# A macaron block (FFN, neighbourhood attention, FFN): the fourth tile's first norm and FFN ahead of the first values, the attention bias's parts earlier, eleven second FFNs held back, and the last norms' products on VectorE

## The chip, the cores and the metric

The kernel runs on one core of one Trainium2 chip. The metric is device time in microseconds (us): of the version before there are three timed runs, 2368.54, 2367.49 and 2367.25, median 2367.49, and one profiled run of 2366.79, whose recorded span is 2365.0. Every duration below comes from that one profiled execution.

A core has a matrix engine (PE in the profile, TensorE), a vector engine (DVE, VectorE), an activation engine (ACT, ScalarE), a general engine (POOL, GpSimd) and a queue that issues transfers (SP, SyncE). Each works through its own list of instructions strictly in order; semaphores tie them together.

## The reference

The input is x, 4 batches of 4096 rows of 512 floats. Cut to what matters:

```python
x = x + 0.5 * ffn(layernorm(x))
x = x + attention(layernorm(x))
x = x + 0.5 * ffn(layernorm(x))

def ffn(x):                     # one 512x512 weight
    xq, xs = mx_quantize(x)     # blocks of 32: scale = max|x|/7.5, values to the FP6-E2M3 grid
    wq, ws = mx_quantize(weight)
    return dequant(xq, xs) @ dequant(wq, ws).T + bias

def attention(x):               # 16 heads of 32, each query sees 13 neighbours
    q, k, v = split(x @ qkv_w.T + qkv_b); q *= 32 ** -0.5
    attn = softmax(q @ k[neighbours].T + rpb[relative position])
    return (attn @ v[neighbours]) @ proj_w.T + proj_b
```

## The kernel before

The 16384 rows are 128 tiles of 128 rows (NT). Four tiles are a group (512 rows), eight groups a batch. What a tile does: load; norm "n1", quantised; first FFN ("f1", its sum in PSUM is pmf); norm "n2"; values (pmv). What a group does, in four items, one for every four heads: queries and keys (pmqk), scores (ps), softmax, probabilities times values (pv), collected in a buffer `ring`. Then each tile again: output projection (pmo); norm "n3", quantised; second FFN ("f2", also pmf); store.

Nearly f32 precision comes from pairs of f16: every operand is kept as a high part and a low part, and `product` (L151) runs three combinations of parts times four chunks of 128, which makes 12 matmuls of 128x512. A high part is a copy on ACT (L200), a low part a subtraction on VectorE (L204), after which SP issues a transposing DMA (L205); xT is what it delivers to the FFN's product.

A quantised norm is made in one stage after another by `quantised_norms`: factors from mean and variance (POOL, L186 to L195), scaled rows y (ACT, L233), block maxima, scales and reciprocals (VectorE, L239 to L244), y times reciprocal (POOL, L246), cast to 8 bits (ACT, L249), times scale (POOL, L251), high part (ACT, L200), low part (VectorE, L204) and transposing DMA. Norms enlisted for the same slot are made as one pair (128x1024 in place of 128x512). For the last tiles a flag `spare`, true from tile 123 on, lets the stage take its buffers from the pool of the tiles (xp, 23 buffers) and not from the norms' own few buffers.

The order is written out by hand. `begin(slot, stage, rank)` puts a stage into a numbered slot, `run_slot` emits a slot's stages by rank, and a stage is a generator that yields how many slots later it goes on. A tile takes STEP = 7 slots; with k = 7t, a tile is loaded at k-18, its norm n1 is enlisted at k-10, `first_half` (first FFN and norm n2) begins at k+5 (F1), `values` at k+20 (V). An attention item takes 7 slots too: pmqk at +38, scores at +42, pv at +59. The output projection of tile t stands at `out_slot(t)`, its norm n3 two slots later, its second FFN at `second_slot(t)`. n1 of tile t and n3 of an earlier tile mostly fall in one slot, and are a pair.

At the start the weights are quantised and transposed ("setup"); 16 chunks of weights are put in place (`put_scaled`, L789 ACT and L791 VectorE, names whl) at listed slots up to 35, and `attention_bias` (its operand vbx at L821 and L822, its product pmb) begins at slot 28. Tiles 0 to 2 have their first norms inside the setup (EARLY = 3); tile 3 is the first whose n1 runs by the slots.

At the end there is too little other work between the last attention items. So eight second FFNs are kept back: HELD (L582) is tiles 113 to 120, and `second_slot` spreads their products over the slots around the last scores and pv. Their transposed operand xT is put in an xp buffer, to wait there. After the last pv come five output projections (tiles 123 to 127) and the last second FFNs.

Of the kernel before, what the change touches and what calls it, by code (L numbers as in the profile page):

```python
# [27 lines left out]
F16 = mybir.dt.float16  # L28
# [4 lines left out]
ALU = mybir.AluOpType  # L33
# [4 lines left out]
P = 128  # L38
# [7 lines left out]
GROUP = 4  # L46
# [4 lines left out]
QB = 32  # L51
# [13 lines left out]
def macaron_kernel(  # L65
# [12 lines left out]
    nc = tc.nc  # L78
# [3 lines left out]
    KC = dim // P  # L82
# [3 lines left out]
    NT = n_batch * length // P  # L86
# [15 lines left out]
    x2p = ctx.enter_context(tc.tile_pool(name="x2p", bufs=2))  # L102
# [17 lines left out]
    half_ffn_b = const.tile([P, dim], F32, name="half_ffn_b")  # L120
# [8 lines left out]
    def bc(t, n):  # L129

        return t.unsqueeze(2).to_broadcast([t.shape[0], t.shape[1], n])
# [30 lines left out]
    def begin(slot, stage, rank=5):  # L162
        slots.setdefault(slot, []).append((rank, stage))
# [19 lines left out]
    def factors(t, which, mv, n=1):  # L183

        rs = sm.tile([P, n], F32, tag=f"rs{which}{n}", name=f"rs{which}_{t}")
        nc.gpsimd.tensor_scalar(  # L186
            rs, mv[:, :n, 1], XS ** -2, LN_EPS * XS ** -2, ALU.mult, ALU.add
        )
        nc.gpsimd.tensor_tensor(rs, rs, minus_half[:, :n], ALU.pow)
        nb = sm.tile([P, n], F32, tag=f"nb{which}{n}", name=f"nb{which}_{t}")  # L190
        if n == 1:
            nc.gpsimd.tensor_scalar(nb, mv[:, 0, 0:1], rs, -1.0, ALU.mult, ALU.mult)  # L192
        else:
            nc.gpsimd.tensor_tensor(nb, mv[:, :n, 0], rs, ALU.mult)
            nc.gpsimd.tensor_scalar(nb, nb, -1.0, None, ALU.mult)  # L195
        return rs, nb

    def high(y, hl):

        nc.scalar.copy(hl[:, :, 0, :], y)  # L200
# [5 lines left out]

    together = {}

    def enlist(slot, t, which):
        together.setdefault(slot, ([], []))[0].append((t, which))
# [7 lines left out]
    def quantised_norms(slot):  # L220

        tiles, mv = together.pop(slot)
        n = len(tiles)
        rs, nb = factors(slot, "q", mv[0], n)
        yield 1, 1

        spare = tiles[0][0] >= NT - GROUP - 1
        if spare:
            y = xp.tile([P, dim], F32, tag="x", name=f"yq{slot}").unsqueeze(1)
        else:  # L230
            y = yp.tile([P, 2, dim], F32, tag="yq", bufs=2, name=f"yq{slot}")[:, :n]
        for u, (t, _) in enumerate(tiles):
            nc.scalar.activation(  # L233
                y[:, u], xs[t], AF.Identity, bias=nb[:, u : u + 1], scale=rs[:, u : u + 1]
            )
        yield 1, 1
        yb = y.rearrange("p u (n q) -> p (u n) q", q=QB)
        sc = sm.tile([P, 2 * NB], F32, tag="sc", bufs=4, name=f"sc{slot}")[:, : n * NB]
        nc.vector.tensor_reduce(sc, yb, AX.X, ALU.max, apply_absolute_value=True)  # L239
        nc.vector.scalar_tensor_tensor(  # L240
            sc, sc, F8_SCALE / Q_MAX, least[:, : n * NB], ALU.mult, ALU.max
        )
        r = sm.tile([P, 2 * NB], F32, tag="r", bufs=4, name=f"r{slot}")[:, : n * NB]
        nc.vector.reciprocal(r, sc)  # L244
        yield 1, 1
        nc.gpsimd.tensor_tensor(yb, yb, bc(r, QB), ALU.mult)  # L246
        yield 1, 1
        q8 = q8p.tile([P, 2, dim], F8, tag="q8", name=f"q8_{slot}")[:, :n]
        nc.scalar.activation(q8, y, AF.Identity, bias=nudge, saturate=False)  # L249
        yield 1, 3  # L250
        nc.gpsimd.tensor_tensor(  # L251
            yb, q8.rearrange("p u (n q) -> p (u n) q", q=QB), bc(sc, QB), ALU.mult
        )
        yield 1, 3
        if spare:
            hl = xp.tile([P, dim], F32, tag="x", name=f"hlq{slot}").bitcast(F16)
            hl = hl.rearrange("p (u s k) -> p u s k", u=1, s=2)
        else:
            hl = hlp.tile([P, 2, 2, dim], F16, tag="hlq", name=f"hlq{slot}")[:, :n]
        high(y, hl)  # L260
        yield 1, 1
        if tiles[0][0] in HELD and tiles[0][1] == "n3":
            xT = xp.tile([P, dim], F32, tag="x", name=f"xT{slot}").bitcast(F16)
            xT = xT.rearrange("p (u s c q) -> p u s c q", u=1, s=2, c=KC)
        else:
            xT = xtp.tile([P, 2, 2, KC, P], F16, tag="xT", name=f"xT{slot}")
        low(y, hl, xT[:, :n].rearrange("p u s c q -> p (u s c) q"))
        for u, (t, _) in enumerate(tiles):
            ys[t] = xT[:, u]
# [11 lines left out]
    def first_half(t):  # L281

        yield from ffn(t, "f1")
        yield 1, 2
        mv = sm.tile([P, 1, 2], F32, tag="mvn2", name=f"mvn2_{t}")
        statistics(t, "n2", mv[:, 0, :])
        yield 1, 2
        rs, nb = factors(t, "n2", mv)
        yield 1, 2
        y = yp.tile([P, 1, dim], F32, tag="yn2", bufs=1, name=f"yn2_{t}")  # L290
        nc.scalar.activation(y[:, 0], xs[t], AF.Identity, bias=nb, scale=rs)
        hl = hlp.tile([P, 1, 2, dim], F16, tag="hln2", name=f"hln2_{t}")
        high(y, hl)
        yield 2, 2
        g, i = divmod(t, GROUP)
        if i == 0:
            x2[g] = x2p.tile([P, 2, KC, GROUP, P], F16, tag="x2", name=f"x2_{g}")
        low(y, hl, x2[g][:, :, :, i, :].rearrange("p s c q -> p (s c) q"))

    x2 = {}  # L300
# [44 lines left out]
    n_items = n_batch * NG * KC  # L345
# [204 lines left out]
    def project_out(t, slot):  # L550

        r = t * P % RING
        pm = ps_m.tile([P, dim], F32, tag="mm", name=f"pmo_{t}")
        product(
            pm, lambda s, c: ring[:, s, c, r : r + P], lambda s, c: wt[:, s, c, PO : PO + dim]
        )
        yield 1, 8
        nc.vector.scalar_tensor_tensor(xs[t], pm, cp, xs[t], ALU.mult, ALU.add)
        moments(slot, t, "n3")
# [7 lines left out]
    EARLY = 3  # L567
    STEP = 7

    F1, V, QK, SC, PV, OUT, F2 = 5, 2 * STEP + 6, 5 * STEP + 3, 6 * STEP, 8 * STEP + 3, 13 * STEP + 2, 12  # L570
# [4 lines left out]
    def one(f, *args):  # L575
        f(*args)
        return
        yield

    HELD = range(NT - 15, NT - 7)  # L582
    LAST = NT - GROUP - 1

    def out_slot(t):


        i = t - LAST
        if i >= 0:
            return (n_items - 1) * STEP + PV + 3 + 2 * i  # L590
        if i >= 1 - GROUP:
            return LAST * STEP + PV + 21 + 4 * i
        return t * STEP + OUT

    def second_slot(t):

        i = t - LAST
        if t in HELD:
            return (n_items - 1) * STEP + PV - (16, 13, 10, 6, 5, 4, 3, 2)[t - HELD[0]]
        if i in (-2, -1):  # L600
            return out_slot(NT - 1) + 3 + i
        return out_slot(t) + F2

    for t in range(NT):
        k = t * STEP
        begin(k - 18, one(load, t), 0)
        enlist(k - 10, t, "n1")
        if not 0 < t < EARLY:
            begin(k - 11, one(moments, k - 10, t, "n1"), 1)
        begin(k + F1, first_half(t))  # L610
        begin(k + V, values(t))
        begin(k + F1, one(add_bias, t, half_ffn_b), 8)
        at = out_slot(t)
        begin(at - 5, one(add_bias, t, after_b), 8)
        enlist(at + 2, t, "n3")
        begin(at, project_out(t, at + 2))
        begin(at + 6 if t < LAST else second_slot(t) - 2, one(add_bias, t, half_ffn_b), 8)
        begin(second_slot(t), second_half(t))
    for slot in together:
        if slot >= EARLY * STEP - 10:  # L620
            begin(slot, quantised_norms(slot), 1)
    for m in range(n_items):
        k = m * STEP
# [3 lines left out]
    for n in range(n_batch * NG):  # L627
        k = n * GROUP * STEP
        b, g = divmod(n, NG)
# [4 lines left out]
    with tc.tile_pool(name="setup", bufs=1) as sp, tc.tile_pool(name="scratch", bufs=2) as scr:  # L634
# [21 lines left out]
        for o in chunks:  # L656
            w, i = (qkv_w, o) if o < 3 * KC else (proj_w, o - 3 * KC)
# [160 lines left out]
        def attention_bias():  # L818

            vbx = sp.tile([P, 2, KC, P], F16, name="vbx")  # L820
            nc.scalar.copy(vbx[:, 0], bc(vb, P))  # L821
            nc.vector.tensor_tensor(vbx[:, 1], bc(vb, P), vbx[:, 0], ALU.subtract)  # L822
            yield 3, 9
            pmb = ps_m.tile([P, dim], F32, tag="mm", name="pmb")
            product(pmb, lambda s, c: vbx[:, s, c, :], lambda s, c: wt[:, s, c, PO : PO + dim])
            yield 1, 9
            nc.vector.scalar_tensor_tensor(after_b, pmb, cp, after_b, ALU.mult, ALU.add)
# [42 lines left out]
        begin(0, one(scales), 9)  # L870
        for slot, o in zip((2, 4, 5, 6, 10, 13, 16, 19, 21, 23, 25, 27, 29, 31, 33, 35), chunks):
            begin(slot, put_scaled(o), 9)
        begin(28, attention_bias(), 9)
        begin(26, one(put_table), 9)
        slot = first
        while slot < QK:
# [47 lines left out]
```

## Time and profile before

| what | value | where it is from |
| --- | --- | --- |
| timed runs | 2367.25, 2367.49, 2368.54 us | median 2367.49 |
| profiled run | 2366.79 us | 0.70 below the median |
| its span | 2365.0 us | 1.79 us of the run lie around it |
| PE not busy | 91.4 us | 2365.0 less 2273.6 busy |
| granted clock of the PE, mean | 0.994 | cores view |
| busy from 120 to 2240 us | PE 99.9% | sum of the stretches in the view by windows |

Times are microseconds from the start of the span. In the view of single instructions a line reads: start, duration, engine, line of the kernel, operation, result<-operands, shape, number of instructions in the row; in brackets the idle time just before it and whose result ended it. In the view by windows a line gives the stretch, its length, then busy time and (in brackets) instructions of PE, PE's weight loads, VectorE, ACT and POOL, then the clock granted to the PE (1.00 is full), the mean busy share of the DMA engines, and GB/s. The chain of waits follows the work that ended last back to the start.

The PE idles in two places only: in the first 106 us, and in the last 105 us.

### The profile page before, as it was taken

How to read it: one execution, taken by the hardware profiler on the slowest of the kernel's cores; microseconds unless marked ns; L12 is line 12 of the kernel's file. 1: busy time of each engine (PE TensorE's matmuls, PEld its weight loads, DVE VectorE, ACT ScalarE, POOL GpSimd, SP SyncE). 2: the span in 40 equal slices, each digit the busy share in tenths (PEclk: the TensorE clock that was granted, in tenths of full speed). 3: DMA queues.
4: the chain of work that ended last, by engine and by line, in shares of the span. 5: the costliest groups of instructions: out<-in, count | busy, mean ns of one | idle time of the engine just before them, and what ended most of it. 6: DMA issues, size and time to landing. Idle time of an engine off the chain costs nothing.

```text
span 2365.0 us, 82328 instructions
## 1 busy us (share of the span) xinstructions
PE 2273.6 (96%) x35539; PEld 1115.4 (47%) x35539; DVE 2022.5 (86%) x3588; ACT 1326.8 (56%) x2080; POOL 1987.6 (84%) x2012
## 2 busy tenths in 40 slices
PE   0799999999999999999999999999999999999988
PEld 0255444444444444444444444444444444444543
DVE  8799888888888888888888888888888888888785
ACT  4466556555555555555555565555555555555542
POOL 5588888888888888888888888888888888888886
PEclk9899999999999999999999999999999999999999
DMA  5789787787777777777777778777777778677763
GB/s 154 146 168 165 156 160 155 147 159 156 151 157 152 156 158 153 156 152 158 153 157 153 153 159 154 153 154 156 158 151 160 151 152 160 153 152 155 133 121 104
DMA packets 925701, 360.59 MB, mean 152 GB/s; under 512 B 718876, under 2 KB 889752, under 8 KB 925336
## 3 DMA queue, kind: packets, MB, share of 16 engines
q1 hardware_dynamic: 924992, 354.79, 73.3%
q8 instruction: 278, 4.55, 0.9%
q10 hardware_dynamic: 344, 0.53, 0.1%
q14 instruction: 87, 0.71, 0.1%
HBM read 110.15 MB, written 67.29 MB: 75 GB/s over the span
## 4 chain that ended last, share of the span: by engine, by line
PE 94%; DVE 3%; DMA 1%; POOL 1%; issue 1%; ACT 0%; SPq 0%; DVEq 0%; ACTq 0%; POOLq 0%
PE pmqk L151 28%; PE pmf L151 27%; PE pmo L151 14%; PE pmv L151 14%; PE ps L442 7%; PE pv L512 3%; DVE fw L761 0%; DMA xT<-hlq 0%; DMA fw<-in_L_ffn_weight_dram 0%; DVE stn L180 0%; DVE wq L763 0%; DVE hlq L204 0%; DVE wqh L757 0%; DMA rows<-in_L_attn_qkv_w_dram 0%; DVE whl L791 0%
## 5 line engine op out<-in xcount | busy, mean ns | idle before, releaser
L151 PE MATMUL pmf<-wt,xT 128*128 128x512 f16 x3048 | 703.5, 381 | 9.1 <-DMA xT<-hlq 9.1
L151 PE MATMUL pmqk<-x,wt 128*128 128x512 f16 x3072 | 705.7, 379 | 1.4 <-DVE vt L315 1.4
L151 PEld LDWEIGHTS <-xT 128*128 128x128 f16 x3048 | 299.1, 98 | 373.7 <-DMA xT<-hlq 11.5
L151 PEld LDWEIGHTS <-wt 128*128 128x128 f16 x3072 | 289.6, 98 | 336.6 <-issue 1.9
L151 PE MATMUL pmv<-wt,x 128*128 128x512 f16 x1536 | 355.0, 381 | 5.1 <-DVE mvn L181 5.1
L246 POOL TENSOR_TENSOR yq<-yq,r 128x1024 f32<-128x1024 f32 (+1 forms) x141 | 246.5, 1748 | 130.0 <-DVE r L244 130.0
L151 PE MATMUL pmo<-wt,ring 128*128 128x512 f16 x1536 | 354.8, 381 | 0.8 <-issue 0.8
L573 POOL TENSOR_TENSOR x<-x,half_ffn_b 128x512 f32<-128x512 f32 x256 | 327.4, 1279 | 0.1
L279 DVE SCALAR_TENSOR_TENSOR x<-pmf,coef,x 128x512 f32<-128x512 f32 x256 | 179.7, 702 | 156.4 <-PE pmf L151 155.9
L314 ACT CAST vt<-pmv 128x512 f16<-128x512 f32 x128 | 74.9, 585 | 388.9 <-PE pmv L151 388.9
L539 ACT ACTIVATE ring<-pv 128x510 f16<-128x510 f32 (+8 forms) x224 | 82.3, 414 | 368.4 <-PE pv L512 368.4
L180 DVE BATCH_NORM_STATS2 stn<-x 128x6 f32<-128x512 f32 x384 | 265.3, 691 | 8.9 <-DMA x<-in_L_attn_x_dram 0.2
L251 POOL TENSOR_TENSOR yq<-q,sc 128x1024 f32<-128x1024 fp8e4 (+1 forms) x141 | 246.7, 1749 | 0.0
L151 PEld LDWEIGHTS <-x 128*128 128x128 f16 x1536 | 150.8, 98 | 188.1 <-DMA x<-hln 5.6
L377 DVE SCALAR_TENSOR_TENSOR qk<-pmqk,qk_b,qk 128x512 f16<-128x512 f32 x256 | 190.5, 744 | 42.2 <-ACT qk L373 41.1
L151 PEld LDWEIGHTS <-ring 128*128 128x128 f16 x1536 | 140.7, 98 | 159.4 <-issue 3.3
L249 ACT ACTIVATE q<-yq,nudge 128x1024 fp8e4<-128x1024 f32 (+1 forms) x141 | 149.9, 1063 | 114.3 <-POOL yq L246 106.1
L485 POOL TENSOR_TENSOR sf<-sf,total 128x714 f32<-128x714 f32 (+2 forms) x128 | 178.6, 1395 | 34.5 <-ACT yq L233 19.1
L373 ACT ACTIVATE qk<-pmqk,qk_b 128x512 f16<-128x512 f32 x256 | 176.1, 688 | 52.1 <-PE pmqk L151 50.8
L186 POOL TENSOR_SCALAR rsq<-mv 128x2 f32<-128x2 f32 (+1 forms) x141 | 130.1, 923 | 89.3 <-DVE mv L181 86.6
L233 ACT ACTIVATE yq<-x,nbq,rsq 128x512 f32<-128x512 f32 x254 | 193.0, 804 | 18.0 <-POOL nbq L192 17.5
L492 POOL TENSOR_TENSOR p<-sf,p 128x714 f16<-128x714 f32 (+2 forms) x128 | 192.6, 1504 | 0.0
(145 smaller groups left out, 3459.7 us busy)
## 6 DMA issues: line engine op xcount, KB each, us to landing
vs<-vd SPq DMA_DIRECT2D x144, 357.0 KB
x<-in_L_attn_x_dram SPq DMA_DIRECT2D x128, 256.0 KB
vd<-vt SPq DMA_DIRECT2D x128, 256.0 KB
out_dram<-x SPq DMA_DIRECT2D x128, 256.0 KB
vs<-vd SPq DMA_DIRECT2D x24, 378.0 KB
vs<-vd SPq DMA_DIRECT2D x24, 315.0 KB
rows<-in_L_attn_qkv_w_dram SPq DMA_DIRECT2D x12, 256.0 KB
xT<-hlq SPq DMA_TRANSPOSE x141
```

Of the source, the lines that this page charges most:

```text
L151: nc.tensor.matmul(pm, lhs(a, c), rhs(b, c), start=(n == 0), stop=(n == 3 * KC - 1))
L180: nc.vector.bn_stats(st, xs[t])
L233: nc.scalar.activation(y[:, u], xs[t], AF.Identity, bias=nb[:, u : u + 1], scale=rs[:, u : u + 1])
L246: nc.gpsimd.tensor_tensor(yb, yb, bc(r, QB), ALU.mult)
L251: nc.gpsimd.tensor_tensor(yb, q8.rearrange("p u (n q) -> p (u n) q", q=QB), bc(sc, QB), ALU.mult)
L279: nc.vector.scalar_tensor_tensor(xs[t], pm, cf, xs[t], ALU.mult, ALU.add)
L373: nc.scalar.activation(t[:, s, 0, KN:], pms[s], AF.Identity, bias=bias)
L377: nc.vector.scalar_tensor_tensor(t[:, s, 1, KN:], pms[s], bias, t[:, s, 0, KN:], ALU.add, ALU.subtract)
L442: nc.tensor.matmul(ps[rows, u, :sides, w * KN : (w + 1) * KN], t[rows, 0, part, q0 : q0 + QR], t[rows, 1, :sides, k0 : k0 + KN], start=par ...
L485: nc.gpsimd.tensor_tensor(s, s, bc(total[:, :n], KN), ALU.mult)
L492: nc.gpsimd.tensor_tensor(p[:, :n, KN : 2 * KN], s, ph, ALU.subtract)
L573: nc.gpsimd.tensor_tensor(xs[t], xs[t], b, ALU.add)
```

## The change

1. Tile 3 is treated like tiles 0 to 2: it is loaded in the same slot as tile 2, its n1 stands at slot 1 and not 11, and the `first_half` of tiles 0 to 3, with the bias additions that belong to it, begins 0, 2, 5 and 7 slots sooner. PE's list then begins pmf0, pmf1, pmf2, pmf3, pmv0, pmv1, pmb, pmf4, pmv2, pmqk0, where it was pmf0, pmf1, pmf2, pmv0, pmf3, pmv1, pmb, pmf4, pmv2, pmqk0. From there on the lists agree until item 119.
2. `attention_bias` makes vbx at slot 20 and not 28; its product stays at slot 31.
3. HELD is tiles 110 to 120, eleven and not eight. Ten of them have new slots around the last pv; tile 120 goes behind all output projections, seven slots after the last. On PE's list the second FFNs of 110, 111 and 112 no longer stand ahead of the scores of items 119, 120 and 121; behind the last scores (item 127) the list reads pmf110, pmo, pv, pmf111, pmo, pmf112, 113, 114, pv, pmf115 to 119, pv, five pmo, pmf121, 122, 123, 124, 120, 125, 126, 127. Before it was pmf113, pmo, pv, pmf114, pmo, pmf115, pv, pmf116 to 120, pv, five pmo, pmf121 to 127.
4. Held tiles from 115 on keep their xT in two buffers of the pool x2p, not in xp.
5. The norm n3 of a held tile is enlisted one slot later, so that it is not paired with an n1 any more. In particular the n1 of tiles 125, 126 and 127 stand alone, and as their first tile is over 122 they count as spare.
6. In spare norms (n1 of 125 to 127, n3 of 123 to 127) the two products, with the reciprocal and with the scale, are made by VectorE and not by POOL.

```diff
+    held = []
...
-        nc.gpsimd.tensor_tensor(yb, yb, bc(r, QB), ALU.mult)
+        mult = nc.vector if spare else nc.gpsimd
+        mult.tensor_tensor(yb, yb, bc(r, QB), ALU.mult)
...
-        nc.gpsimd.tensor_tensor(
+        mult.tensor_tensor(
             yb, q8.rearrange("p u (n q) -> p (u n) q", q=QB), bc(sc, QB), ALU.mult
         )
...
-        if tiles[0][0] in HELD and tiles[0][1] == "n3":
+        t0 = tiles[0][0]
+        is_held = t0 in HELD and tiles[0][1] == "n3"
+        if is_held and t0 >= NT - 13:
+            g, i = divmod(t0 - (NT - 13), GROUP)
+            if i == 0:
+                held.append(x2p.tile([P, 2, KC, GROUP, P], F16, tag="x2", name=f"held{g}"))
+            xT = held[g][:, :, :, i, :].unsqueeze(1)
+        elif is_held:
...
-    HELD = range(NT - 15, NT - 7)
+    HELD = range(NT - 18, NT - 7)
...
+        if t == HELD[-1]:
+            return out_slot(NT - 1) + 7
         if t in HELD:
-            return (n_items - 1) * STEP + PV - (16, 13, 10, 6, 5, 4, 3, 2)[t - HELD[0]]
+            return (n_items - 1) * STEP + PV - (16, 13, 10, 9, 8, 6, 5, 4, 3, 2)[t - HELD[0]]
...
     for t in range(NT):
         k = t * STEP
-        begin(k - 18, one(load, t), 0)
-        enlist(k - 10, t, "n1")
+        sooner = (0, 2, 5, STEP)[t] if t <= EARLY else 0
+        begin(k - 18 - (STEP if t == EARLY else 0), one(load, t), 0)
+        slot = k - 10 - (10 if t == EARLY else 0)
+        enlist(slot, t, "n1")
         if not 0 < t < EARLY:
-            begin(k - 11, one(moments, k - 10, t, "n1"), 1)
-        begin(k + F1, first_half(t))
+            begin(slot - 1, one(moments, slot, t, "n1"), 1)
+        begin(k + F1 - sooner, first_half(t))
         begin(k + V, values(t))
-        begin(k + F1, one(add_bias, t, half_ffn_b), 8)
+        begin(k + F1 - sooner, one(add_bias, t, half_ffn_b), 8)
         at = out_slot(t)
         begin(at - 5, one(add_bias, t, after_b), 8)
-        enlist(at + 2, t, "n3")
-        begin(at, project_out(t, at + 2))
+        n3 = at + (3 if t in HELD else 2)
+        enlist(n3, t, "n3")
+        begin(at, project_out(t, n3))
...
     for slot in together:
-        if slot >= EARLY * STEP - 10:
+        if together[slot][0][0][1] == "n3" or together[slot][0][0][0] >= EARLY:
             begin(slot, quantised_norms(slot), 1)
...
-            yield 3, 9
+            yield 11, 9
...
-        begin(28, attention_bias(), 9)
+        begin(20, attention_bias(), 9)
```

## The prediction

> **What bounds the kernel now.** First the page: busy time and the chain.
>
> ```profile
> PE 2273.6 (96%) x35539; PEld 1115.4 (47%) x35539; DVE 2022.5 (86%) x3588; ACT 1326.8 (56%) x2080; POOL 1987.6 (84%) x2012
> PE 94%; DVE 3%; DMA 1%; POOL 1%; issue 1%; ACT 0%; SPq 0%; DVEq 0%; ACTq 0%; POOLq 0%
> ```
>
> PE sets the end, and the two programs give it equally many instructions. So only PE's 91.4 us of idleness and its cold stretches can be had. The view by windows says where they are:
>
> ```profile
> 20.00:40.00 20.00, 0.37 (x1) 0.08 (x1) 20.00 (x31) 7.24 (x19) 15.81 (x12) 1.00 0.18 54
> 80.00:100.00 20.00, 12.45 (x41) 4.66 (x42) 18.23 (x33) 10.29 (x16) 10.84 (x17) 0.74 0.80 165
> 2260.00:2280.00 20.00, 17.79 (x415) 9.21 (x415) 15.71 (x32) 9.37 (x15) 17.76 (x17) 0.91 0.56 101
> 2300.00:2320.00 20.00, 15.33 (x131) 6.79 (x130) 14.22 (x24) 7.03 (x13) 18.47 (x18) 0.83 0.72 168
> ```
>
> From 20 to 40 VectorE is full (20.00 of 20.00, setup); at 80 PE has 12.45 of 20 and a clock of 0.74; near the end it idles again. PE's own timeline names each wait:
>
> ```profile
> 72.92 5.30 PE L151 MATMUL pmv<-wt,x 128*128 128x512 f16 x12 [5.10 <-DVE mvn L181]
> 82.49 4.24 PE L151 MATMUL pmf<-wt,xT 128*128 128x512 f16 x12 [4.27 <-DMA xT<-hlq]
> 86.56 2.75 PE L151 MATMUL pmv<-wt,x 128*128 128x512 f16 x12
> ...
> 98.80 2.94 PE L151 MATMUL pmf<-wt,xT 128*128 128x512 f16 x12
> ...
> 2272.20 1.34 PE L442 MATMUL ps<-qk 32*32 32x84 f16 x144 [2.15 <-DVE qk L377]
> 2273.48 4.42 PE L151 MATMUL pmo<-wt,ring 128*128 128x512 f16 x12
> ...
> 2306.32 0.83 PE L512 MATMUL pv<-pT,vs 126*32 126x30 f16 x72 [4.67 <-DMA vs<-vd]
> ...
> 2351.39 9.63 PE L151 MATMUL pmf<-wt,xT 128*128 128x512 f16 x36 [2.53 <-DMA xT<-hlq]
> ```
>
> A warm product (12 matmuls) takes 2.60 from start to start, 4.2 to 5.3 behind an idle spell. The last two items wait 2.14 and 2.15 for VectorE's low part of the keys, pv then 4.67, and the last FFNs 0.39, 1.93 and 2.53.
>
> **The head.** Tile 3's norm joins the setup. By the starts of a later tile's rows (moments 64.00, 64.72, 64.82; maximum, scale, reciprocal 70.22, 70.93, 71.14, 71.31) that is 0.72 + 0.10 + 0.71 + 0.21 + 0.17 = 1.9 on the full VectorE, and 1.55 where instructions of other work stand between these, since a 512-wide one then takes 0.6 from start to start. Its low part (0.60) falls into the 6.22 in which VectorE waits for pmf0 (56.4 to 62.67), its two products into POOL's free 4.2 of the stretch from 20 to 40. The setup is interleaved, so pmf0 comes 1.5 later; at least 0.6 (some falls behind 40, where VectorE has 3.7 of 20 free), at most 2.5 (dependent steps, and the low part in front of pmf0 after all: 1.9 + 0.6). SP issues one more transpose and one earlier load there; its queue is not what pmf0 waits for (that is the weights' transposing).
>
> Then pmf3 follows pmf2 at once and no longer stands in pmv0's and pmv1's way. Before, its xT came at 82.49 (L204 at 77.43, 1.76 long, then 3.3 for the transpose). I lay the same instructions out in the new lists, with the durations of their rows: pmv0 still at 73, pmv1 78.6 (was 86.56), x3 complete at 82.0 (was 92.58), pmb 87.5, bound by the last projection weights (was 90.51 and 95.41: vbx is now early, so the 1.19 and 3.86 for it go), the low part for pmf4 at 89.5 and pmf4 at 94.05 (was 98.80: 4.75 sooner). Behind it pmqk0 at 99.4 (105.73) and first scores at 110.5 (116.18): 5.7 sooner. I take 4.7, as pmf4's own, since pmqk0 also needs tile 3's n2 chain. vbx moved eight slots ahead costs VectorE 0.6 ahead of x2's moments, already in the layout. Net: 1.5 - 4.7 = -3.2 (-5.1 to 0). From 116 to 2170 PE has no wait to speak of, so all of it is carried through.
>
> **The tail, first part.** Without pmf110, 111, 112 three periods of an item hold 15.0 of PE's work, not 17.6: 3 x 2.60 = 7.8 to gain. VectorE must keep up. It had 15.44 of 17.59; it loses the FFN's addition (0.66) and a slow pair's low part (1.89, as two alone 1.20), gains two products (2 x 0.60) and a pair's small steps apart (2 x 1.10 for 1.74): 15.44 - 0.66 - 0.69 + 1.20 + 0.46 = 15.75, above 15.0. The first period keeps an addition more (0.67), a fourth has 13.1. So 61.0 of VectorE against 62.6 of PE over four, and up to 64.5 where POOL's tensor operations stand in the way; with 2.1 from the last low part to the scores that would be 66.6. I take the middle, 2.4 of the 7.8 lost: -5.4 (-7.8 to 0).
>
> The products on VectorE have rows only by their nearest kin, the 512-wide subtraction:
>
> ```profile
> 2254.02 1.51 DVE L204 TENSOR_TENSOR hlq<-yq,hlq 128x512 f16<-128x512 f32 x1
> ...
> 2266.11 0.67 DVE L204 TENSOR_TENSOR hlq<-yq,hlq 128x512 f16<-128x512 f32 x1
> ```
>
> The first ran beside a POOL subtraction begun at 2253.52 (1.46); the second began 0.07 before POOL's next, which then took 1.92. Whoever comes second pays: 0.67 or about 1.5 for a product that took POOL 1.05.
>
> The Trainium skill ("GPSIMD Engine Reference", Specifications) says GpSimd's SBUF interfaces are shared with VectorE, with contention where a VectorE instruction has two SBUF inputs. It speaks against moving products to VectorE while POOL still adds biases; taken whole, all five additions in the last stretch (1.24 each) would be in front of a product there, 6.2 on the uncontended -0.7 of the last stretch below, 5.5 in place of my 2.0, span 2364.6; the rows show it only for some pairs.
>
> **The tail, held norms.** A held tile's norm is a slot later, so its high copy (ACT, L200, 0.52) and low part (VectorE, 0.60) enter the chain pv, ring, high of queries, low, sum, low of keys, scores: 1.12 per period. Two periods of 12.4 have 0.45 to spare: +0.67 each; the two with waits of 2.14 and 2.15 pay 1.12 each; the last (14.28) 0.8. Sum 4.4 (3.6 where the two without waits absorb it, 6 with one more cold spell of 1.7, the 4.42 for 2.76). Split pairs put three more transposes on SP's queue; behind one that waits for its low part stand vs's loads and a store. Nothing but pv and the end waits for these, and in the layout vs comes 3.0 ahead of PE, which is their cover; without it pv would be later by the 0.6 to 1.5 of a low part. The two buffers of x2p are last read by item 123's and 127's projections; the first is free before tile 115's low part, so no wait; if not, VectorE's whole list would stand there, one item's period of 12.4 at most.
>
> **From the last scores to the five pmo** (2286.48 to 2322.71, 36.2): two more products (5.2) go where pv waits 4.67 and PE is cold (2.0): 36.2 + 5.2 - 4.67 - 2.0 = 34.7; -1.7 in my layout, where vs is there at 2304.8 and PE arrives at 2307.8.
>
> **From there to the last product** (38.3): one more product (2.60) fills the waits of 4.85, and VectorE makes ten products beside POOL's five additions. Uncontended 37.6; with every second addition in the way 40 to 41.3. I take +2.0 (-0.7 to +3). The last addition (0.9) and the store (3.1) stay.
>
> Here the clock matters: by the Trainium skill ("TensorE: Matmul & The Clock Gate", HAM oscillation — how this bites in real kernels) only idle gaps over some 3.4 us are to be avoided. The trace has a cold product behind 2.15 (the 4.42 above), so short waits are not free here; by the rule 1.7 would go from my held-norm bound.
>
> **Sum.** Head -3.2; tail -5.4 + 4.4 - 1.7 + 2.0 = -0.7. Together -3.9: span 2365.0 to 2361.1. The profiled run is 2366.79, and the median 0.70 above it; the same difference from 2367.49 gives 2363.5.
>
> **Rivals.** (1) VectorE keeps up: the head as above (-3.2), 7.8 won whole, held norms at their lower 3.6, -1.7, the end at 0: -9.1, 2358.4. For it: 61.0 of VectorE's work against 62.6. Against: 61.0 of 62.6 is 97%, and its fullest long stretch in the middle, 200 to 250, has 47.0 of 50. (2) Slower: VectorE in order becomes the bound from item 119 on. Its products meet POOL's subtractions and take 1.5 each; from 17.6 of its work in a 15.0 period on nothing of the 7.8 is left, and the held norms' copies, in the same chain, cost their upper 6: 0 + 6 - 1.7 + 3 at the end, head -1.5: +5.8, 2373.3. It decides from two contended products per period on (15.75 + 2 x 0.9 = 17.55). For it: POOL is at 17.76 of 20 in that stretch. Against: the row of 0.67, and POOL loses six products of 1.05 there. That the change does not do what it says is excluded by the lists of instructions, which show the three FFNs gone from before items 119 to 121. (3) The head brings nothing: 2.5 of delay in setup, and pmqk0 bound by tile 3's n2 chain, only 2.5 sooner; then -0.7 of the tail alone, 2366.8. For it: the head's VectorE is at 18.23 of 20 already. Against: the two waits of 5.10 and 4.27 and the cold clock of 0.74, with nothing else behind them than pmf3's place.
>
> **Chances.** Forecast 0.48 (its own range 2361 to 2366), (1) 0.27, (2) 0.12, (3) 0.13. What a measurement of this kernel can tell from no change is 0.2%, 4.7 us: faster is below 2362.8, slower above 2372.2. (1) is faster, as is the lower part (0.15) of the forecast: 0.42. (2) is slower: 0.12. The rest 0.46. The range 2358 to 2371 takes in (1)'s centre, (3), the unknown contention, and leaves out (2).
>
> **What would show it.** Right: pmf3 within 3 of pmf2, first scores near 112.5, PE idle before them 3 less; no wait of 4.67 ahead of a pv; pv to scores 1.1 longer in the last five items; products by VectorE at L246 and L251 of 0.6 to 1.5. Wrong: pmf0 later than 61; waits for VectorE ahead of items 119 to 122; a wait above 3 in the last FFNs; hidden held copies.

## The result, and the profile after

The changed kernel takes 2376.68 us (median of six runs, 2374.64 to 2377.66) where the kernel before takes 2368.48 in the same comparison: a ratio of 1.0032, 95% interval 1.0019 to 1.0045, so 0.3% slower. The forecast was 2363.5 with a range to 2371; the second rival, the slower one, had 2373.3. The profiled execution has a span of 2375.0, 10.0 longer than before.

The page of the changed kernel, busy time and chain:

```profile
PE 2275.2 (96%) x35539; PEld 1116.5 (47%) x35539; DVE 2037.4 (86%) x3616; ACT 1327.3 (56%) x2086; POOL 1978.4 (83%) x2008
PE 89%; DVE 6%; issue 1%; ACT 1%; DMA 1%; POOL 1%; SPq 0%; DVEq 0%; ACTq 0%; POOLq 0%
```

PE is busy as long as before; VectorE's share of the chain went from 3% to 6%. PE's waits over the whole run (us in total, times, longest):

```profile
...
PE ps L451 <- DVE qk L386: 13.2, 7, 3.3
PE pmf L151 <- DMA xT<-hlq: 8.1, 3, 4.4
...
PE pmv L151 <- DVE qk L386: 5.1, 4, 2.6
...
PE pmb L151 <- ACT yn L300: 4.2, 1, 4.2
...
PE pv L521 <- DMA vs<-vd: 1.1, 1, 1.1
```

The old waits did go: the 4.67 for vs ahead of a late pv is no longer there (the 1.1 left is at 142 us), the two of pmb for its operand vbx neither (it now waits 4.2, with ACT's scaled rows of a norm n2 as the last event before it). A new one stands first behind two waits of the setup, 25.9 and 16.6 (26.8 and 15.2 before): scores wait seven times for VectorE's low part of the keys (L386, the old L377), 13.2 in all where it was 4.3. The windows say where:

```profile
2150.00:2200.00 50.00, 44.34 (x782) 21.77 (x781) 47.72 (x83) 24.48 (x41) 33.45 (x40) 0.97 0.58 114
...
2340.00:2360.00 20.00, 14.13 (x59) 5.75 (x57) 19.45 (x34) 6.02 (x9) 11.50 (x14) 0.91 0.19 54
```

From 2150 to 2200, where PE was never idle before, it now has 44.34 of 50, VectorE 47.72 (41.97 before), GpSimd 33.45 (43.71). Between 2340 and 2360 it is likewise VectorE that is nearly full, 19.45 of 20 (11.99 before), and GpSimd that has less, 11.50 (13.94). PE's timeline in the tail:

```profile
2171.53 1.28 PE L451 MATMUL ps<-qk 32*32 32x84 f16 x136 [1.27 <-DVE qk L386]
...
2191.14 1.27 PE L451 MATMUL ps<-qk 32*32 32x84 f16 x136 [2.40 <-DVE qk L386]
2192.35 4.44 PE L151 MATMUL pmo<-wt,ring 128*128 128x512 f16 x12
...
2264.36 2.08 PE L451 MATMUL ps<-qk 32*32 32x84 f16 x144 [3.27 <-DVE qk L386]
...
2356.68 4.20 PE L151 MATMUL pmf<-wt,xT 128*128 128x512 f16 x12 [4.35 <-DMA xT<-hlq]
```

Where the 10.2 us up to the last product come from is seen when the starts of the same products are set side by side. This table holds the time from one stretch's end to the next, in us, read off the PE timelines of the profiled executions (ps119 is the start of item 119's scores; "five" the start of the five output projections):

| stretch | before | changed | difference |
| --- | --- | --- | --- |
| start to ps118 | 2155.39 | 2155.19 | -0.2 (at the first scores it was -2.5) |
| ps118 to ps122, three FFNs taken out | 67.77 | 69.58 | +1.8 |
| ps122 to ps127 | 63.32 | 70.14 | +6.8 |
| ps127 to five | 36.23 | 34.84 | -1.4 |
| five to the end of the last product | 38.31 | 41.48 | +3.2 |

The three periods of the second row are 16.34, 19.61 and 18.64 long (17.59 each before); the fourth step in it has 14.99 (15.00). The -0.2 of the first row can't be read as what the head is worth: the long middle differs by more than that between profiled executions of equal lists (see the last section).

### The profile page after: what moved, and what is told of

Its sections match the earlier page's. It is cut to its first block, busy times and chain, and to the rows that moved or that the text cites. A ratio compares the mean times of both kernels' runs of the same rounds, so it can differ in the third digit from the quotient of the medians.

```text
span 2375.0 us, 82379 instructions
## 1 busy us (share of the span) xinstructions
PE 2275.2 (96%) x35539; PEld 1116.5 (47%) x35539; DVE 2037.4 (86%) x3616; ACT 1327.3 (56%) x2086; POOL 1978.4 (83%) x2008
## 4 chain that ended last, share of the span: by engine, by line
PE 89%; DVE 6%; issue 1%; ACT 1%; DMA 1%; POOL 1%; SPq 0%; DVEq 0%; ACTq 0%; POOLq 0%
PE pmf L151 27%; PE pmqk L151 27%; PE pmo L151 14%; PE pmv L151 13%; PE ps L451 6%; PE pv L521 3%; DVE hlq L204 1%; DVE qk L386 1%; DVE stn L180 0%; DVE sc L240 0%; DVE total L490 0%; DVE fw L775 0%; DVE hln L204 0%; DVE whl L805 0%; ACT yn L300 0%
## 5 line engine op out<-in xcount | busy, mean ns | idle before, releaser
L151 PE MATMUL pmf<-wt,xT 128*128 128x512 f16 x2976 | 683.5, 380 | 9.6 <-DMA xT<-hlq 8.1
L151 PEld LDWEIGHTS <-xT 128*128 128x128 f16 x2976 | 290.9, 98 | 363.1 <-DMA xT<-hlq 12.4
L248 POOL TENSOR_TENSOR yq<-yq,r 128x1024 f32<-128x1024 f32 (+1 forms) x136 | 239.1, 1758 | 137.8 <-DVE r L245 131.6
L253 POOL TENSOR_TENSOR yq<-q,sc 128x1024 f32<-128x1024 fp8e4 (+1 forms) x136 | 238.2, 1752 | 8.8 <-ACT q L251 8.8
L386 DVE SCALAR_TENSOR_TENSOR qk<-pmqk,qk_b,qk 128x512 f16<-128x512 f32 x256 | 190.4, 744 | 47.0 <-ACT qk L382 45.9
```

The costliest lines, as they stand in the source:

```text
L151: nc.tensor.matmul(pm, lhs(a, c), rhs(b, c), start=(n == 0), stop=(n == 3 * KC - 1))
L248: mult.tensor_tensor(yb, yb, bc(r, QB), ALU.mult)
L253: mult.tensor_tensor(yb, q8.rearrange("p u (n q) -> p (u n) q", q=QB), bc(sc, QB), ALU.mult)
L386: nc.vector.scalar_tensor_tensor(t[:, s, 1, KN:], pms[s], bias, t[:, s, 0, KN:], ALU.add, ALU.subtract)
```

## The experiments

Every run gives its median and its ratio to the kernel before, measured on the same chip beside it. Line numbers in the rows of a variant are its own and can differ by some from the changed kernel's.

**The two halves alone.** The head alone is the kernel before with the first and second part of the change:

```diff
 # kernel before, plus
+        sooner = (0, 2, 5, STEP)[t] if t <= EARLY else 0
...
+        begin(20, attention_bias(), 9)
```

> The kernel before with the head of the change alone (tile 3's norm and FFN sooner, the attention bias's operand sooner). The two traces show the first scores 2.48 us sooner in the changed kernel, and only 0.7 left of it at 234 us, after waits for VectorE's low part of the keys. Theory: the gain is paid back there whatever the tail does, so -0.7 (0 to -1.5), some 2367.8 for a before of 2368.5. Rival: the loss between 116 and 234 us is chance, the whole -2.5 stays, 2366.0.

2366.45, ratio 0.9992 (0.9984 to 1.0001): -1.3, inside the theory's range; by its interval it can't be told from no change. Where the gain goes is taken up below ("The head"): it is not only waits for the low part of the keys. The tail alone is the changed kernel with these parts undone:

> The kernel before with the tail of the change alone (eleven FFNs held, their norms a slot later, last norms' products on VectorE). If the parts add up, all of the loss is here: +8 to +10.5, 2377 to 2379 for a before of 2368.5. Rival: the two parts hinder each other (the tail's list starts from another phase), then it is nearer to +5.

2378.14, ratio 1.0042 (1.003 to 1.0055), +10.4 over that comparison's 2367.77. The whole loss is in the tail, and the parts add up within their intervals (-1.3 and +10.4 against +8.2).

**Products back on GpSimd.**

```diff
-        mult = nc.vector if spare else nc.gpsimd
+        mult = nc.gpsimd
```

> The changed kernel with all products of the norms back on GpSimd. Theory A: VectorE is full in the three periods in front of items 119 to 121 because two products per period came to it; then these periods fall from 16.3, 19.6 and 18.6 us to some 15.5 and the last stretch loses its +3.2: -6 to -9 against the changed kernel, about 2369. Rival B: the pairs made apart fill VectorE, not the products: -1 to -3, about 2375.

2368.57, ratio 1.0003 (0.9994 to 1.0012): 8.1 less than the changed kernel (7.4 if each is set against the kernel before that ran beside it; the stretches of the two profiles differ by 7.0, of which 3.0 in the periods and 4.0 in the last). The time was forecast by theory A, its place only in part: the last stretch falls from 41.48 to 37.49 as said, but the three periods become 15.03, 18.46 and 18.07, not 15.5. Something besides the products holds them up.

**The later slot only where pairs are parted.**

```diff
-        n3 = at + (3 if t in HELD else 2)
+        n3 = at + (3 if t in HELD[:3] else 2)
```

> The changed kernel, but only the norms of tiles 110 to 112 are a slot later (they have a pair to be parted from); those of 113 to 120 stand where they stood before the change. Theory: the slot puts their high copy and low part into the chain of the last scores, which cost 0.86 + 1.11 + 2.34 + 1.80 = 6.1 us over four periods; that goes: -4 to -6, about 2371.5. Rival: those periods are long because VectorE is behind from the three periods ahead of them: within 1 us of the changed kernel.

2372.65, ratio 1.0022 (1.0013 to 1.0031): 4.0 less than the changed kernel (3.3 if each is set against the kernel before that ran beside it). The five steps from ps122 to ps127 are 12.58, 12.44, 12.11, 13.69 and 14.17, in sum 65.0 and not 70.1 (63.3 before). That the slot lengthened these steps is shown; in this run's profile the stretches behind them give 2.8 of the 5.1 back. The changed kernel's own rows show the two intruders, first ACT's list:

```profile
2272.95 0.66 ACT L548 ACTIVATE ring<-pv 128x12 f16<-128x12 f32 x2 [5.36 <-PE pv L521]
2273.50 0.62 ACT L200 CAST hlq<-yq 128x512 f16<-128x512 f32 x1
2274.00 0.70 ACT L382 ACTIVATE qk<-pmqk,qk_b 128x512 f16<-128x512 f32 x1
```

and VectorE's:

```profile
2274.74 0.75 DVE L386 SCALAR_TENSOR_TENSOR qk<-pmqk,qk_b,qk 128x512 f16<-128x512 f32 x1 [3.27 <-ACT qk L382]
2275.41 0.74 DVE L554 SCALAR_TENSOR_TENSOR ring<-pv,ring 128x12 f16<-128x12 f32 x2
2276.07 0.68 DVE L204 TENSOR_TENSOR hlq<-yq,hlq 128x512 f16<-128x512 f32 x1
2276.67 0.93 DVE L490 TENSOR_REDUCE total<-sf 128x18 f32<-128x756 f32 x1
...
2278.03 0.74 DVE L386 SCALAR_TENSOR_TENSOR qk<-pmqk,qk_b,qk 128x512 f16<-128x512 f32 x1
```

From ring to the queries' high part 0.50 go to the norm's copy (2273.50 to 2274.00), from ring to total 0.60 to its subtraction. PE waits for the last line here. Before, both stood elsewhere: the copy in front of pv's result, the subtraction in front of the first low part.

**Pairs kept.** Holding a tile needs its transposed operand in a place of its own, and the change got that by parting its norm from the pair. It is enough to part the transposing DMA:

```diff
-        n3 = at + (3 if t in HELD else 2)
+        n3 = at + 2
...
+            nc.vector.tensor_tensor(hl[:, :, 1, :], y, hl[:, :, 0, :], ALU.subtract)
+            for u in range(n):
+                dst = xT[:, u] if where[u] is None else where[u]
+                nc.sync.dma_start_transpose(
+                    out=dst.rearrange("p s c q -> p (s c) q"),
+                    in_=hl[:, u].rearrange("p s k -> p (s k)"),
+                )
```

> The changed kernel with all products on GpSimd, no norm later than before, and the pairs of tiles 110 to 112 with 125 to 127 kept: one norm of 128x1024, only the transposing DMA is issued for each tile by itself, the held tile's to its waiting place. Theory: the pairs parted, the products on VectorE and the later slot are the whole loss, and holding eleven FFNs is a gain without them. VectorE then has 15.44 - 0.66 = 14.8 us in a period of 15.0: the periods of items 119 to 121 are 15.0 to 15.5 (-6.5 to -7.8), the four last periods as before, -1.4 from the last scores to the five output projections, -0.8 behind them, -1.3 the head: -10 to -11, 2357 for a before of 2367.8. Rival: VectorE is the bound there in any case (its waits are not to be packed into 15.0), periods of 16.5 to 17.5: -4 or less, 2363 or more.

2359.33, ratio 0.9962 (0.9949 to 0.9974): faster than both kernels. The three periods are 15.00, 15.00 and 15.80, the theory's numbers but for the last, which is 0.3 above them. The whole is 2.3 above the forecast, in the two stretches behind: 64.6 from ps122 to ps127 (63.3 before) and 36.3 from there to the five (forecast 34.8); the last has 37.5, as forecast. Its head is the changed kernel's.

**Both partial undoings together.** It differs from the last one in the parted pairs and what came with the parting in the change: the norms n3 of 110 to 112 stand a slot later, and the n1 of 125 to 127 use the buffers of the spare norms. The products are on GpSimd in both.

> The changed kernel with products on GpSimd and only the norms of tiles 110 to 112 later: the two partial undoings together. If they are separate costs, -8.1 and -4.0 add up: 2364.6. If both take from one and the same VectorE load, less than their sum: 2367 or more.

2365.18, ratio 0.9989 (0.998 to 0.9997): the sum of the two gains, within 0.6. Against the version with pairs it is 5.9 slower, and the periods show why: 15.01, 18.41 and 18.04. The rows of the second period on which this rests, with parted pairs (scores at 2170.69):

```profile
2176.53 1.04 POOL L253 TENSOR_TENSOR yq<-q,sc 128x512 f32<-128x512 fp8e4 x1
2177.61 0.72 ACT L251 ACTIVATE q<-yq,nudge 128x512 fp8e4<-128x512 f32 x1 [2.73 <-POOL yq L253]
2180.30 1.17 DVE L204 TENSOR_TENSOR hlq<-yq,hlq 128x512 f16<-128x512 f32 x1 [0.98 <-ACT hlq L200]
2184.43 1.65 DVE L204 TENSOR_TENSOR hlq<-yq,hlq 128x512 f16<-128x512 f32 x1
2186.00 0.88 DVE L490 TENSOR_REDUCE total<-sf 128x17 f32<-128x714 f32 x1
2187.22 1.17 DVE L492 TENSOR_TENSOR total<-total,p_scale 128x17 f32<-128x17 f32 x1
2188.31 0.74 DVE L386 SCALAR_TENSOR_TENSOR qk<-pmqk,qk_b,qk 128x512 f16<-128x512 f32 x1
```

and with pairs kept (scores at 2168.98):

```profile
2175.86 1.42 DVE L282 TENSOR_TENSOR hlq<-yq,hlq 128x1024 f16<-128x1024 f32 x1 [0.34 <-ACT hlq L200]
2181.47 0.30 DVE L504 TENSOR_TENSOR total<-total,p_scale 128x17 f32<-128x17 f32 x1
2181.70 0.74 DVE L398 SCALAR_TENSOR_TENSOR qk<-pmqk,qk_b,qk 128x512 f16<-128x512 f32 x1
```

The last line of each is the low part of the keys, for which PE waits 2.39 in the one and not at all in the other. It stands 17.62 behind the scores with parted pairs, 12.72 with pairs: 4.9 later. VectorE has no gap from the norm's low part (the first DVE line) to it in either, so the 4.9 are two things. That stretch of VectorE's list is 8.01 and not 5.84 long: two low parts take 2.65 from start to start where the pair's one takes 1.34, and the scaling of the total takes 1.09 and not 0.23. And the stretch begins 9.61 and not 6.88 behind the scores, since VectorE has to wait 0.98 for ACT's copy of the norm. ACT is late because of the cast (the ACT line), which stands ahead of its copies. The cast's operand was ready at 2174.08, but the cast begins at 2177.61, right behind GpSimd's product for the other norm of the two: that product reads q, and the pool of q (`q8p`) has one buffer, so the second norm can't be cast before the first has been read. A pair is cast once, in one buffer. GpSimd's product itself ends 6.88 behind the scores, 1.1 later than the pair's (5.77). All three periods with parted pairs have this wait (2.29, 2.73, 2.73; in the changed kernel 3.70, 2.22, 2.21 for VectorE's product). How much of the 5.9 is the single buffer, how much the later slot and how much the doubled instructions no run here separates: none gives `q8p` a second buffer.

VectorE's share of busy time does not tell the two apart: in the second period it is 17.08 of 18.41 with parted pairs (93%) and 14.38 of 15.00 with pairs (96%). The sum does, 2.7 more.

**Products on VectorE behind the last pv alone.** As with pairs kept, with the `mult` line of the change: VectorE has the ten products of tiles 123 to 127 and no others.

> As e_pairs_kept, but the products of the last five norms (tiles 123 to 127) on VectorE, ten products and no others. The stretch behind the five output projections was 41.5 with these products on VectorE and 37.5 without: if VectorE's own list in that stretch is the cause, +4 against e_pairs_kept; if a backlog from the periods ahead was, within 1 us of it.

2364.7, ratio 0.9986 (0.9977 to 0.9995): +5.4, the last stretch 42.52 against 37.47. It is the stretch itself, not a backlog. In the changed kernel VectorE's rows in this stretch are

```profile
2350.53 1.57 DVE L248 TENSOR_TENSOR yq<-yq,r 128x512 f32<-128x512 f32 x1
2352.02 1.75 DVE L204 TENSOR_TENSOR hlq<-yq,hlq 128x512 f16<-128x512 f32 x1
2353.69 1.75 DVE L253 TENSOR_TENSOR yq<-q,sc 128x512 f32<-128x512 fp8e4 x1
```

beside this row of GpSimd, which has no products left to wait for and runs the five bias additions as one burst:

```profile
2350.28 7.50 POOL L582 TENSOR_TENSOR x<-x,half_ffn_b 128x512 f32<-128x512 f32 x5
```

**The burst left out.** As the last one, and the additions of the FFN's bias to the last five tiles are missing, so their output lacks it:

```diff
-        begin(at + 6 if t < LAST else second_slot(t) - 2, one(add_bias, t, half_ffn_b), 8)
+        if t < LAST:
+            begin(at + 6, one(add_bias, t, half_ffn_b), 8)
```

> As g_pairs_kept_vector, with GpSimd's additions of the FFN's bias for the last five tiles left out (their output lacks that bias). In the changed kernel these five run as one burst of 7.50 us, and VectorE's products and subtractions beside it take 1.57, 1.75 and 1.75 where 0.7 is usual. Theory: it is this contention that makes the last stretch 42.5 with products on VectorE: without the additions 38 to 39, the whole 2360 to 2361 where g_pairs_kept_vector had 2364.7. Rival: VectorE's own list, with ten instructions more, is the bound, contended or not: 41.5 or more, within 1.2 us of g_pairs_kept_vector.

2360.23, ratio 0.9969 (0.9957 to 0.9981), 4.5 less than the last one; the last stretch is 39.73, between the two ranges and nearer to the theory's. The same three rows:

```profile
2335.59 0.68 DVE L248 TENSOR_TENSOR yq<-yq,r 128x512 f32<-128x512 f32 x1
2336.19 0.68 DVE L204 TENSOR_TENSOR hlq<-yq,hlq 128x512 f16<-128x512 f32 x1
2336.79 0.68 DVE L253 TENSOR_TENSOR yq<-q,sc 128x512 f32<-128x512 fp8e4 x1
```

So of the 5.05 that the products on VectorE cost there, 2.8 (42.52 - 39.73) go with the burst; the other 2.3 stay, and are taken to be the longer list of VectorE itself, which has no gap over 0.3 from 2328.5 to 2341.8. That part is read off the rows, no run takes it away by itself.

**The head: what pays its gain back.** In the changed kernel the first scores wait for nothing, but pmv just ahead of them waits 2.60 for VectorE, and pv at 142 us waits for vs, the values that come through memory:

```profile
111.02 2.75 PE L151 MATMUL pmv<-wt,x 128*128 128x512 f16 x12 [2.60 <-DVE qk L386]
...
142.40 0.63 PE L521 MATMUL pv<-pT,vs 126*32 126x30 f16 x60 [1.06 <-DMA vs<-vd]
```

Of the 2.48 won at the first scores 2.11 are left at the third (137.30 against 139.41) and 0.89 at the fourth, behind this pv (150.83 against 151.72). In the run with the head alone nothing was won to begin with: the same pmv is cold behind its wait,

```profile
111.68 4.44 PE L151 MATMUL pmv<-wt,x 128*128 128x512 f16 x12 [2.59 <-DVE qk L377]
```

the first scores come at 116.04 (116.18 before), and pv finds vs there. Of the nine profiles here with the head and otherwise equal lists up to the tail, three are cold at this pmv and six wait 0.5 to 2.5 for vs. Their item 9's scores stand at 232.40 to 235.68, in mean at 233.87; those of the three without the head at 233.85 to 234.78, in mean at 234.30. So little of the 2.5 is left by then.

A first attempt moved four low parts of weights to GpSimd, two instructions each:

```diff
+            if o in (0, 1, 2, 3):
+                nc.gpsimd.tensor_scalar(rows[o], rows[o], s, None, ALU.mult)
+                nc.gpsimd.tensor_tensor(hl[:, 1, :], rows[o], hl[:, 0, :], ALU.subtract)
+            else:
```

> The kernel before with the head of the change, and the low parts of four of the sixteen weight chunks (those at slots 21, 25, 29 and 33) made by GpSimd in two instructions each and not by VectorE in one of 0.66 us. Theory: from 80 to 150 us VectorE's list is the bound in every kernel here, so PE's sooner start is paid back; 4 x 0.66 = 2.6 less of it make item 9's scores, and the end, 1.5 to 2.6 sooner than with the head alone: 2364 to 2365 where that was 2366.45. Rival: the way of the values through memory (pv waits 1.1 to 2.5 us for vs at 142 us) is the bound: no change, 2366.5.

2370.21, ratio 1.001 (1.0001 to 1.0019): neither forecast, 3.8 slower than the head alone. GpSimd's two take 1.57 to 1.94 and 1.15 to 1.45 and stand in front of the norms' products, for which VectorE then waits in turn (up to 2.65 for a copy that follows them). It tells nothing on VectorE's load. The second attempt takes the load away without giving it to anybody of weight:

```diff
+            if o in (0, 1, 2, 3):
+                nc.gpsimd.memset(hl[:, 1, :], 0.0)
+            else:
```

> The kernel before with the head of the change; the low parts of four weight chunks (slots 21, 25, 29, 33) are left out, GpSimd clears their place (their products lose those digits). It takes 4 x 0.66 = 2.6 us from VectorE without the two long GpSimd instructions for each that stood in front of the norms in h_head_lows_gpsimd. Theory: VectorE's own list is the bound from 80 to 150 us: item 9's scores at 231 to 232.3 and not 233.7, the end 1.5 to 2.6 below the head alone, 2364 to 2365. Rival: the chain of the norms over GpSimd, ACT and VectorE is the bound there, not VectorE's load: within 0.7 of the head alone, 2366.5.

2364.19, ratio 0.9983 (0.9974 to 0.9992): 2.3 below the head alone, though the two intervals overlap. Item 9's scores are at 231.04, ahead of all nine profiles with the head and 2.8 ahead of their mean: about the 2.6 that were taken from VectorE between 80 and 107 us, as the theory has it. The wait of 2.60 is 1.47 here, pmv is warm, and pv finds vs there at 140.44. This points to VectorE's list as what lies ahead of both waits; that the wait for vs would go with it was not forecast:

```profile
109.90 2.75 PE L151 MATMUL pmv<-wt,x 128*128 128x512 f16 x12 [1.47 <-DVE qk L377]
```

**Tile 120 sooner, and the head in the best version.** With pairs kept, tile 120's product moves ahead of tile 124's (`out_slot(NT - 1) + 5` and not `+ 7`):

> As e_pairs_kept, with the second FFN of the held tile 120 two slots earlier: ahead of tile 124's, where PE waits 1.99 us for its transposed operand, and not behind it. Theory: the product fills the wait: -1.5 to -2, 2357.5 where e_pairs_kept had 2359.3. Rival: behind it the next operand is late in turn, the end is set by VectorE and GpSimd in that stretch: no change.

2358.21, ratio 0.9958 (0.9944 to 0.9971): 1.1 below, within what the intervals leave open, and the stretch is 37.10 against 37.47. The wait of 1.99 is filled and 1.49 and 0.89 stand behind it: nearer to the rival. The same without the head of the change:

> As j_120_before_124, without the head of the change. If the head is worth its measured 1.3 us: 2358.8. If that was chance: as j_120_before_124 within 0.7 us.

2360.08, ratio 0.9965 (0.9952 to 0.9977): 1.9 more. With the head alone at -1.3 this points to a gain of one to two us, but neither interval excludes none.

## Why the prediction was wrong, step by step

- **"The tail, first part", -5.4, is the step that failed:** +1.8. The uncontended sum of VectorE's work, 15.75 per period, was about right: the second period, 19.61, is VectorE's list from one low part of the keys to the next, with one gap of 0.32; 15.9 of it are uncontended distances from start to start, the other 3.7 are four instructions beside GpSimd's (1.13, 1.80 and 1.58 in place of 0.60 for low parts, 1.09 in place of 0.10 for the scaling of the total). The term that was too small is "where POOL's tensor operations stand in the way": I gave it 3.5 in four periods, and it is 3.7 in one. The comparison beside it was wrong as well. If its four periods are those of the second row of the table, they hold 67.8 - 7.8 = 60.0 of PE's work and not 62.6, so VectorE's 61.0 was the longer list before any contention. And no term stood for a second norm whose cast waits for the first, with ACT's copies and VectorE's low parts behind it. The bound of 66.6 for the four periods became 69.58. Pairs kept, they take 60.8; parted, 66.6 (+5.8, products on GpSimd); with the products on VectorE besides, 69.6 (+3.0).
- **"The head", -3.2:** the delay of pmf0 (0.8, 58.99 against 58.23) and the first scores (-2.5) are near the sum, but "all of it is carried through" was wrong: the sum followed PE's waits before the change, which end at 106 us. With PE's list moved up there are new ones behind it, for VectorE at 111 and for vs at 142, or a cold product in their place. At item 9's scores 0.7 was left.
- **"Held norms", +4.4:** right in mechanism and in its 1.12 where an item was already waiting (13.21 against 12.10); in sum +6.8, above the bound of 6, of which the later slot alone has 5.1. The terms that were small were those with slack: 0.71 and 0.86 in place of 0.67, 2.34 for the second with a wait and 1.80 in place of 0.8 for the last, with cold matmuls in them (2.08 for scores that take 1.34).
- **"From the last scores to the five pmo", -1.7:** -1.4 in the changed kernel, where the rows are as the layout had them: the two products fill the 4.67, and all are warm. It was in part luck. With the scores on time the stretch is 36.33 (pairs kept), as before: PE then arrives earlier and waits 0.68 and 0.49 for VectorE's additions, which the layout did not have.
- **"From there to the last product", +2.0:** +3.2, just above the upper bound of 3. Contention with the bias additions was the right cause for the larger part (2.8 of 5.05 go with them where pairs are kept); that GpSimd, rid of its products, runs them in a burst was not foreseen. The Trainium skill ("GPSIMD Engine Reference", Specifications) says that GpSimd's SBUF interfaces are shared with VectorE, with contention where a VectorE instruction has two SBUF inputs. The rows agree: beside the burst products and subtractions, which have two, take 1.57 to 1.75 and a block maximum, which has one, 0.67 (at 2356.02).
- **The rivals.** The second had place and engine: the periods from item 119 on, all 7.8 lost, the held copies at their upper end, +3 at the end; 2373.3 against 2376.68, the difference mostly the head, of which it had -1.5, and the periods, which it had at nothing lost. Its price per period was put on the products alone, which the runs show to be the smaller part. The chance of 0.12 was too low: that VectorE's sum for a period lay above PE's was in the forecast's own working. The third, that the head brings nothing, is nearer to what is left of the head than the forecast, but not by its mechanism: pmf0 came 0.8 later and not 2.5.

## What to carry to other kernels

Work that leaves the bounding engine gains only until the next in-order list is full, so lay out that list, with its contended durations, before counting the gain. An engine's share of busy time does not show it: here a period grew by 3.4 us while VectorE's share fell. If a buffer's lifetime forces an operand into a place of its own, try to part the transfer and not the computation: keeping the pair, with its slot, was worth 5.9 us here, and with the old slots and the old engine besides, a loss of 8 became a gain of 8.6. Before a pair is parted, count the buffers of every pool that its two halves then need at once. An engine that is relieved of its waits runs its remaining work in bursts, and what it shares with its neighbour is then contended all at once.

## What was not expected of the hardware

Contention goes down to the smallest instructions: GpSimd's last factor of a norm, one value per partition, takes 0.77 where it begins within 0.02 of a product of VectorE (2341.42 and 2345.44) and 0.27 beside VectorE's addition of an FFN's sum, which reads PSUM (2350.06), all in the changed kernel's last stretch.

PE ran cold behind a wait of 2.40, 5 us after another of 2.00 (an output projection of 4.44 where 2.76 is usual), so waits under 3 us can cost another 1.7. They need not: with the tail alone the same two waits are 2.39 and 1.88, and the product behind them takes 2.76.

Between profiled executions the long middle drifts: two versions whose lists agree to item 118 (tile 120 behind or ahead of tile 124) have its scores at 2153.98 and 2157.28. A difference of a few us between two spans is no verdict; steps inside a stretch repeat to some hundredths, except where a product or scores run cold (13.50 and 13.78 for the step from item 125's scores to item 126's in the same two).
